# Attention on the array's sixteen squares: ten orders and divisions in place of one

## The chip, the cores and the metric

The kernel runs on one core of one Trainium2 chip. The metric is the device time of one execution in microseconds; shown is the median of three runs. Engines are called as in the profile: PE is the matrix engine (PEld its weight loads), DVE, ACT and POOL are the three element-wise engines, SP issues most of the DMAs.

## The reference

Cross attention with two sets of keys. There are 2 batches of 2048 tokens with 640 channels (20 heads of 32 channels), and per batch 154 context rows of 1024 channels: 77 text rows and 77 image rows. All numbers are float32.

```python
q = split_heads(x @ Wq.T, 20)
k, v = split_heads(text @ Wk.T, 20), split_heads(text @ Wv.T, 20)
out_text = merge_heads(softmax(q @ k.T / sqrt(32)) @ v)
k_ip, v_ip = split_heads(ip @ Wk_ip.T, 20), split_heads(ip @ Wv_ip.T, 20)
out_ip = merge_heads(softmax(q @ k_ip.T / sqrt(32)) @ v_ip)
return (out_text + out_ip) @ Wo.T + bo + x
```

## The kernel before

The 640 channels are five chunks of 128, and a chunk holds four heads. Chunk and batch together give ten numbers q = 0 to 9 (batch 0 first). For each q the kernel makes queries (`queries`, L201), scores of every token against the 154 keys of both sets (`scores`, L233), two softmaxes per head on DVE, POOL and ACT (`take` to `normalise`), a transpose of 32 x 32 blocks in place (`transpose`, L323), and then the weighted sum of the values on PE: `attend` (L332), called by the word `A.q` of the schedule. `take_attention` (word `CA.q`, L355 and L359, on ACT) copies its result from PSUM to the tile `aT`. The output projection (L471, L490, L500, L848) works on `aT`, for batch 0 beside the attention of batch 1, for batch 1 after it.

The order of all this is written out by hand, word by word, in `SCHEDULE`; each engine runs its own instructions in that order, and semaphores make it wait for the others. Nothing in the build chooses another order.

`attend` sees the PE array as sixteen squares of 32 rows and 32 columns. Square (r, g) works for head g of the chunk and for a quarter r of the tokens: its weights are the values `v4s[q % 2]` (tile `v`) of one key block, 32 keys by 32 channels, its moving operand are the probabilities of those keys in `pb` for 512 tokens (16 groups of 32 tokens), and it writes partitions 32g to 32g+31 of PSUM bank `pa[r]`. The 154 keys are padded to 160, five key blocks k = 0 to 4, which a square adds up in the same place of PSUM. That is 5 x 16 = 80 matmuls a call. A float32 matmul is run in two passes, each with its own weight load: four instructions (load, pass, load, pass), and two records of each kind in the profile. The 80 matmuls stand with the key block outermost, then the row r, then the column g ("by row").

The schedule gives each call half of the eight PSUM banks (`A.0@1` takes banks 4 to 7); their earlier contents must have been read by ACT or DVE before the first matmul that writes a bank.

Of the kernel before, what the change touches and what calls it, by code (L numbers as in the profile page):

```python
# [15 lines left out]
H, D, TEXT = 20, 32, 77  # L16
# [4 lines left out]
def kernel(  # L21
# [25 lines left out]
    nc = tc.nc  # L47
# [3 lines left out]
    G = P // D  # L51
# [9 lines left out]
    NK = (2 * L + D - 1) // D  # L61
# [28 lines left out]
    v4s = [const.tile([P, G, NK, D], F32, name=f"v4_{n}") for n in range(2)]  # L90
# [234 lines left out]
    def attend(q, pa):  # L325

        zones = pb[:, ds(q % 2, SUB)].rearrange("p z n g (k s) -> p (z n) g k s", k=NK)
        for k in range(NK):
            for r in range(G):
                rows = slice(r * D, (r + 1) * D)  # L330
                for g in range(G):
                    nc.tensor.matmul(  # L332
                        pa[r][g * D : (g + 1) * D, :],
                        v4s[q % 2][rows, g, k, :],
                        zones[rows, :, g, k, :],
                        start=(k == 0),
                        stop=(k == NK - 1),
                    )

    def rows_of_attention(b, c):  # L340

# [290 lines left out]
    def emit(word):  # L632
# [7 lines left out]
        elif k == "A":  # L640
            at[name] = halves[int(where)]
            attend(x, at[name])
        elif k == "CA":
            take_attention(x, at[f"A.{x}"])
# [246 lines left out]
```

## Time and profile before

| | us |
|---|---|
| median of three runs (497.68 to 497.79) | 497.76 |
| span of the profiled execution, first to last instruction | 496.7 |
| PE busy in it | 490.3 |
| PEld busy | 287.9 |
| DVE busy | 408.5 |
| POOL busy | 362.5 |
| ACT busy | 315.0 |
| `attend` (L332), PE busy, ten calls | 55.2 |

The profiled execution shows its span alone; the 1.06 us between the span and the median lie outside the instructions, and differences are reckoned against the median as they stand.

A profile line gives the source line, the engine, the operation and the tiles (`bank<-pb,v` reads pb and v and writes a bank). [...] "x160" counts records, so 160 are 80 matmuls. A weight load's line is PEld. In the view of stretches, each stretch has the busy time of an engine, and in brackets how many records lie in it or reach into it.

### The profile page before, as it was taken

Reading aid. Unit: us, or ns where it says so; the run is one execution under the profiler, and the core shown is the slowest. Engines: PE = TensorE matmul, PEld = TensorE weight load, DVE = VectorE, ACT = ScalarE, POOL = GpSimd, SP = SyncE. Lnnn points to the kernel's source line nnn. Section 1 sums busy time; section 2 is a strip of 40 time slices with the busy share of each in tenths; the row PEclk is TensorE's granted clock in tenths of the full one; section 3 lists DMA queues with packets and bytes.
Section 4 is the critical chain, followed back from the end, with each engine's and each line's share of the span. In section 5 each row is a group of like instructions: output and inputs, shape, how many; then the busy total and the mean of one; then the engine's idle time right before and its main releaser. Section 6 shows DMA issues by size and latency. Waiting matters only on the chain.

```text
span 496.7 us, 10482 instructions
## 1 busy us (share of the span) xinstructions
PE 490.3 (99%) x4114; PEld 287.9 (58%) x4114; DVE 408.5 (82%) x412; ACT 315.0 (63%) x1021; POOL 362.5 (73%) x157
## 2 busy tenths in 40 slices
PE   8999999999999999999999999999999999999997
PEld 5676657657547556456647654755755675444442
DVE  0069989979979989969976896687999978898877
ACT  1165878978978778668999786587578966100000
POOL 0069978798888999989874858565899888284830
PEclk9999999999999999999999999999999999999999
DMA  8991440332360454886445177418525401420115
GB/s 259 356 246 40 132 120 1 106 93 69 92 213 3 132 178 132 274 273 237 158 152 191 58 244 210 133 57 246 174 69 171 127 23 43 149 84 1 43 73 223
DMA packets 67474, 69.38 MB, mean 140 GB/s; under 512 B 5473, under 2 KB 47201, under 8 KB 67425
## 3 DMA queue, kind: packets, MB, share of 16 engines
q1 hardware_dynamic: 66704, 68.00, 43.8%
q8 instruction: 32, 0.52, 0.5%
q10 hardware_dynamic: 720, 0.72, 0.4%
q14 instruction: 18, 0.14, 0.1%
HBM read 54.94 MB, written 10.49 MB: 132 GB/s over the span
## 4 chain that ended last, share of the span: by engine, by line
PE 92%; DMA 3%; SPq 1%; DVE 1%; POOL 1%; ACT 1%; issue 0%; POOLq 0%
PE bank L201 33%; PE bank L848 11%; PE bank L490 10%; PE bank L233 10%; PE bank L332 10%; PE bank L142 9%; PE bank L471 6%; PE bank L500 3%; DMA aT<-in_L_xattn_Wk_ip_dram 2%; DMA wq<-in_L_xattn_Wq_dram 2%; SPq L534 1%; POOL pb L316 1%; DVE den L306 0%; ACT pb L301 0%; SPq L132 0%
## 5 line engine op out<-in xcount | busy, mean ns | idle before, releaser
L316 POOL TENSOR_TENSOR pb<-pb,rden 128x1848 f32<-128x1848 f32 (+1 forms) x60 | 176.1, 2944 | 39.7 <-DVE rden L311 35.5
L201 PE MATMUL bank<-x,wq 128*128 128x512 f32 x400 | 180.4, 601 | 0.6 <-DMA x<-in_x_dram 0.5
L295 POOL TENSOR_TENSOR pb<-pb,mx 128x1848 f32<-128x1848 f32 (+1 forms) x38 | 119.3, 3152 | 51.8 <-DVE mx L281 51.5
L201 PEld LDWEIGHTS bank<-x,wq 128*128 128x128 f32 x400 | 74.1, 191 | 86.7 <-issue 80.8
L323 DVE STREAM_TRANSPOSE pb<-pb 128x1920 f32<-128x1920 f32 (+1 forms) x60 | 115.7, 1932 | 4.9 <-POOL pb L316 4.3
L281 DVE TENSOR_REDUCE mx<-pb 128x24 f32<-128x1848 f32 (+1 forms) x51 | 93.7, 1850 | 30.7 <-ACT pb L245 30.5
L245 ACT COPY pb<-bank 128x462 f32<-128x462 f32 (+1 forms) x204 | 87.2, 539 | 36.0 <-PE bank L233 35.4
L306 DVE TENSOR_REDUCE den<-pb 128x24 f32<-128x1848 f32 (+1 forms) x47 | 88.7, 1895 | 17.6 <-ACT pb L301 13.3
L301 ACT ACTIVATE pb<-pb 128x1848 f32<-128x1848 f32 (+1 forms) x38 | 64.2, 1696 | 17.8 <-POOL pb L295 17.5
L269 ACT ACTIVATE pb<-pb,mx 128x77 f32<-128x77 f32 x224 | 67.8, 364 | 0.3 <-DVE mx L281 0.2
L233 PEld LDWEIGHTS bank<-kT,qT 32*128 32x128 f32 x1280 | 45.4, 184 | 26.9 <-issue 15.6
L269 ACT ACTIVATE pb<-bank,mx 128x77 f32<-128x77 f32 x184 | 51.8, 386 | 9.3 <-DVE mx L284 9.3
L233 PE MATMUL bank<-kT,qT 32*128 32x154 f32 x1280 | 56.2, 305 | 0.3 <-ACT kT L559 0.3
L332 PE MATMUL bank<-pb,v 32*32 32x512 f32 x1600 | 55.2, 597 | 0.0
L142 PE MATMUL bank<-wo_ct,aT 128*128 128x154 f32 x320 | 45.6, 296 | 0.3 <-DMA aT<-in_L_xattn_Wk_ip_dram 0.3
L142 PEld LDWEIGHTS bank<-wo_ct,aT 128*128 128x128 f32 x320 | 42.9, 188 | 3.6 <-issue 2.2
L332 PEld LDWEIGHTS bank<-pb,v 32*32 32x32 f32 x1600 | 29.9, 103 | 22.8 <-issue 10.7
L211 ACT ACTIVATE qT<-bank 128x512 f32<-128x512 f32 x40 | 24.2, 619 | 22.1 <-PE bank L201 22.0
L471 PE MATMUL bank<-aT,wo_ct 128*128 128x512 f32 x80 | 36.1, 596 | 0.0
L269 ACT ACTIVATION_READ_ACCUMULATOR pb<-bank,mx 128x1 f32 x128 | 33.6, 267 | 0.0
L490 PE MATMUL bank<-aT,wo_ct 128*128 128x256 f32 x128 | 32.3, 385 | 0.0
L490 PEld LDWEIGHTS bank<-aT,wo_ct 128*128 128x128 f32 x128 | 23.7, 190 | 6.5 <-issue 3.0
(75 smaller groups left out, 434.4 us busy)
## 6 DMA issues: line engine op xcount, KB each, us to landing
x<-in_x_dram SPq DMA_DIRECT2D x20, 1280.0 KB, 6.7
out_dram<-acc SPq DMA_DIRECT2D x20, 256.0 KB, 2.3
x<-in_x_dram SPq DMA_DIRECT2D x18, 256.0 KB, 5.9
acc<-in_x_dram SPq DMA_DIRECT2D x16, 256.0 KB, 4.7
out_dram<-x SPq DMA_DIRECT2D x15, 256.0 KB, 2.0
v<-vS SPq DMA_DIRECT2D x160, 20.0 KB, 2.8
wq<-in_L_xattn_Wq_dram SPq DMA_DIRECT2D x9, 320.0 KB, 5.0
aT<-in_L_xattn_Wk_dram SPq DMA_DIRECT2D x5, 512.0 KB, 5.5
```

Of the source, the lines that this page charges most:

```text
L142: nc.tensor.matmul(keys_in(out), loaded[n][:, k, :], cT[:, k, :, t, :], start=(k == 0), stop=(k == NCC - 1))
L201: nc.tensor.matmul(pq, wqs[q % 3][:, k, :], xs[place_of(u, h)][:, k, :], start=(k == 0), stop=(k == NC - 1),)
L233: nc.tensor.matmul(ps[g][:, ts(t, 2 * L)], qTs[(u, h)][g * D : (g + 1) * D, ts(st, P)], kT[g * D : (g + 1) * D, c, b].rearrange("p t l -> ...
L245: nc.scalar.copy(keys_of(u, s)[:, :, g], ps[g][:, : n * 2 * L].rearrange("p (n l) -> p n l", n=n))
L269: nc.scalar.activation(row, row if ps is None else rows_in(ps[g], n)[:, t, x], AF.Exp, bias=maxs[(u, s)][:, *one], accum_out=None if den i ...
L281: nc.vector.tensor_reduce(mx, rows_of(u, s), AX.X, ALU.max, negate=negate)
L295: nc.gpsimd.tensor_tensor(rows_of(u, s), rows_of(u, s), maxs[(u, s)].unsqueeze(3).to_broadcast([P, n, 2, L]), ALU.subtract)
L306: nc.vector.tensor_reduce(den_of(u, s), rows_of(u, s), AX.X, ALU.add)
L316: nc.gpsimd.tensor_tensor(rows_of(u, s), rows_of(u, s), rdens[(u, s)].unsqueeze(3).to_broadcast([P, n, 2, L]), ALU.mult)
L323: nc.vector.transpose(p, p)
L332: nc.tensor.matmul(pa[r][g * D : (g + 1) * D, :], v4s[q % 2][rows, g, k, :], zones[rows, :, g, k, :], start=(k == 0), stop=(k == NK - 1),)
L490: nc.tensor.matmul(part, w_of[m][:, kp, op], t_of(m, b, i)[:, kp], start=(op == kp == 0 and m in (1, 2, 5)), stop=(op == 1 and kp == 1 and ...
```

## The change

Only `attend` is changed. Each q has its own entry of a table: an order of the sixteen squares (`byrow`, `bycol`, `diagonal`), and for each of the sixteen a number `first`. Where `first` is 32, the first key block is one matmul as before. Where it is between 2 and 32, the square's matmul of the first key block covers only the first `first` tokens of each group of 32 tokens, and the others follow as a matmul of their own after the last key block. Where it is 2, the two pieces (2 and 30 tokens of each group) follow each other at once. All sixteen squares still run every key block in the table's order. The products and sums are the same.

```diff
     def attend(q, pa):
 
         zones = pb[:, ds(q % 2, SUB)].rearrange("p z n g (k s) -> p (z n) g k s", k=NK)
-        for k in range(NK):
-            for r in range(G):
-                rows = slice(r * D, (r + 1) * D)
-                for g in range(G):
-                    nc.tensor.matmul(
-                        pa[r][g * D : (g + 1) * D, :],
-                        v4s[q % 2][rows, g, k, :],
-                        zones[rows, :, g, k, :],
-                        start=(k == 0),
-                        stop=(k == NK - 1),
-                    )
+        byrow = [(r, g) for r in range(G) for g in range(G)]
+        bycol = [(r, g) for g in range(G) for r in range(G)]
+        diagonal = [((d + g) % G, g) for d in range(G) for g in range(G)]
+        order, first = (
+            (byrow, [12 + i for i in range(16)]),
+            (bycol, [12 + i for i in range(16)]),
+            (byrow, [12 + 2 * (i // 2) for i in range(16)]),
+            (byrow, [D, 2] + [D] * 14),
+            (bycol, [D] * 16),
+            (diagonal, [12 + i for i in range(16)]),
+            (byrow, [D, 2] * 8),
+            (byrow, [16 + i // 2 for i in range(16)]),
+            (bycol, [12 + i // 4 * 5 for i in range(16)]),
+            (byrow, [12 + i // 4 * 5 for i in range(16)]),
+        )[q]
+
+        def part(k, i, lo, hi, start, stop):
+            r, g = order[i]
+            rows = slice(r * D, (r + 1) * D)
+            nc.tensor.matmul(
+                pa[r][g * D : (g + 1) * D, :].rearrange("p (n s) -> p n s", s=D)[:, :, lo:hi],
+                v4s[q % 2][rows, g, k, :],
+                zones[rows, :, g, k, lo:hi],
+                start=start,
+                stop=stop,
+                skip_group_check=True,
+            )
+
+        for i in range(G * G):
+            part(0, i, 0, first[i], True, False)
+            if first[i] == 2:
+                part(0, i, 2, D, False, False)
+        for k in range(1, NK):
+            for i in range(G * G):
+                part(k, i, 0, D, False, False)
+        for i in range(G * G):
+            if 2 < first[i] < D:
+                part(0, i, first[i], D, False, True)
```

A call of q = 0, 1, 2, 5, 7, 8 or 9 has 96 matmuls now, that of q = 6 has 88, that of q = 3 has 81 and that of q = 4 has 80. The other engines run the same instructions in the same order. The rows below are PE's instructions in program order, with what each waits for; `bank_71` to `bank_74` are PSUM banks 4 to 7, `v_0_80` and `v_1_81` are the two value tiles, `32x512` is a moving operand of 32 partitions and 512 columns, `32x16x12` one of 16 groups of 12.

The first key block of the call q = 0, before: sixteen whole matmuls by row.

```order
L332 MATMUL bank_71<-pb,v_0_80 32x512 [waits DMAHW0_49,DVE_49,Activation_49]
L332 MATMUL bank_71<-pb,v_0_80 32x512 [waits DMAHW4_49]
L332 MATMUL bank_71<-pb,v_0_80 32x512 [waits DMAHW6_49]
L332 MATMUL bank_71<-pb,v_0_80 32x512 [waits DMAHW2_49]
L332 MATMUL bank_72<-pb,v_0_80 32x512 [waits DMAHW1_49,Activation_49]
L332 MATMUL bank_72<-pb,v_0_80 32x512 [waits DMAHW5_49]
L332 MATMUL bank_72<-pb,v_0_80 32x512 [waits DMAHW7_49]
L332 MATMUL bank_72<-pb,v_0_80 32x512 [waits DMAHW3_49]
L332 MATMUL bank_73<-pb,v_0_80 32x512 [waits DMAHW2_49,Activation_49]
```

The same place now:

```order
L347 MATMUL bank_71<-pb,v_0_80 32x16x12 [waits DMAHW0_49,DVE_49,Activation_49]
L347 MATMUL bank_71<-pb,v_0_80 32x16x13 [waits DMAHW4_49]
L347 MATMUL bank_71<-pb,v_0_80 32x16x14 [waits DMAHW6_49]
L347 MATMUL bank_71<-pb,v_0_80 32x16x15 [waits DMAHW2_49]
L347 MATMUL bank_72<-pb,v_0_80 32x16x16 [waits DMAHW1_49,Activation_49]
L347 MATMUL bank_72<-pb,v_0_80 32x16x17 [waits DMAHW5_49]
L347 MATMUL bank_72<-pb,v_0_80 32x16x18 [waits DMAHW7_49]
L347 MATMUL bank_72<-pb,v_0_80 32x16x19 [waits DMAHW3_49]
L347 MATMUL bank_73<-pb,v_0_80 32x16x20 [waits DMAHW2_49,Activation_49]
```

Squares and waits stand where they stood; each matmul covers 12 to 27 columns of every 32.

The end of the call q = 1, before: the last key block by row, and then the scores that follow.

```order
L332 MATMUL bank_71<-pb,v_1_81 32x512 x4
L332 MATMUL bank_72<-pb,v_1_81 32x512 x4
L332 MATMUL bank_73<-pb,v_1_81 32x512 x4
L332 MATMUL bank_74<-pb,v_1_81 32x512 x4
L233 MATMUL bank_67<-kT,qT_0_752 128x154 [waits Activation_49]
```

The same place now:

```order
L347 MATMUL bank_74<-pb,v_1_81 32x16x9
L347 MATMUL bank_71<-pb,v_1_81 32x16x8
L347 MATMUL bank_72<-pb,v_1_81 32x16x7
L347 MATMUL bank_73<-pb,v_1_81 32x16x6
L347 MATMUL bank_74<-pb,v_1_81 32x16x5
L233 MATMUL bank_67<-kT,qT_0_768 128x154 [waits Activation_49]
```

What the first key block left out comes last, sixteen short matmuls in the order by column; five of these rows are shown.

The start of the call q = 6, before:

```order
L332 MATMUL bank_71<-pb,v_0_80 32x512 [waits DVE_49,Activation_49]
L332 MATMUL bank_71<-pb,v_0_80 32x512 [waits DMAHW1_49]
L332 MATMUL bank_71<-pb,v_0_80 32x512 x2
L332 MATMUL bank_72<-pb,v_0_80 32x512 [waits DMAHW6_49,Activation_49]
L332 MATMUL bank_72<-pb,v_0_80 32x512
```

The same place now:

```order
L347 MATMUL bank_71<-pb,v_0_80 32x512 [waits DVE_49,Activation_49]
L347 MATMUL bank_71<-pb,v_0_80 32x16x2 [waits DMAHW1_49]
L347 MATMUL bank_71<-pb,v_0_80 32x16x30
L347 MATMUL bank_71<-pb,v_0_80 32x512
L347 MATMUL bank_71<-pb,v_0_80 32x16x2
L347 MATMUL bank_71<-pb,v_0_80 32x16x30
L347 MATMUL bank_72<-pb,v_0_80 32x512 [waits DMAHW6_49,Activation_49]
```

Every second square has two matmuls one behind the other, and the first key block is 24 matmuls.

## The prediction

> **What bounds the kernel now.** The page first, for the engine that sets the end:
>
> ```profile
> span 496.7 us, 10482 instructions
> ...
> PE 490.3 (99%) x4114; PEld 287.9 (58%) x4114; DVE 408.5 (82%) x412; ACT 315.0 (63%) x1021; POOL 362.5 (73%) x157
> ...
> PE 92%; DMA 3%; SPq 1%; DVE 1%; POOL 1%; ACT 1%; issue 0%; POOLq 0%
> ...
> L332 PE MATMUL bank<-pb,v 32*32 32x512 f32 x1600 | 55.2, 597 | 0.0
> ```
>
> PE is busy for 490.3 of 496.7 us and carries 92% of the chain that ended last; the four lines before the last are its start. Next PE's row of waits, longest and shortest of five:
>
> ```profile
> PE bank L549 <- DVE pb L547: 1.1, 1, 1.1
> ...
> PE bank L490 <- DVE acc L515: 0.2, 1, 0.2
> ```
>
> The five sum to 2.2 us. So a microsecond that `attend` takes more or less on PE is a microsecond of the span, as long as PE waits for nobody else, and L332 holds 55.2 us. Third, inside one call (q = 2): the timeline of PE and of its weight loads.
>
> ```profile
> 143.97 5.52 PE L332 MATMUL bank<-pb,v 32*32 32x512 f32 x160
> 149.41 0.81 PE L233 MATMUL bank<-kT,qT 32*128 32x154 f32 x16
> ```
>
> ```profile
> 143.96 0.23 PEld L332 LDWEIGHTS bank<-pb,v 32*32 32x32 f32 x32 [0.76 <-ACT vT L688]
> 144.42 0.10 PEld L332 LDWEIGHTS bank<-pb,v 32*32 32x32 f32 x1 [0.23 <-issue]
> 144.85 0.55 PEld L332 LDWEIGHTS bank<-pb,v 32*32 32x32 f32 x32 [0.32 <-issue]
> 145.71 2.87 PEld L332 LDWEIGHTS bank<-pb,v 32*32 32x32 f32 x95 [0.30 <-issue]
> ```
>
> A call takes 5.52 us of PE. What could it take? The pace of a pass stands in these rows (two windows of PE):
>
> ```profile
> 248.53 6.17 PE L201 MATMUL bank<-x,wq 128*128 128x512 f32 x14
> ```
>
> ```profile
> 387.26 1.03 PE L490 MATMUL bank<-aT,wo_ct 128*128 128x256 f32 x4
> ```
>
> ```profile
> L332 PE MATMUL bank<-pb,v x1600: 584/587/612, 69.8 to 428.6; 32*32 32x512 f32 x178
> ```
>
> Fourteen passes of 512 columns: (6.17 - 0.59 for the last one's record) / 13 = 0.429 us each; four of 256 columns: (1.03 - 0.38) / 3 = 0.217. A pass costs by its columns with nearly nothing fixed, and a matmul, two passes, 1.676 ns per column: 0.858 us for 512. Were no square ever idle, five key blocks would take 5 x 0.858 = 4.29 us and not 5.52. Where the difference lies, the loads tell, counted by stretch over the same call:
>
> ```profile
> 143.96:144.40 0.44, 0.23 (x32) 1.00 1.10 360
> 144.40:144.80 0.40, 0.10 (x1) 1.00 1.12 347
> 144.80:145.02 0.22, 0.10 (x1) 1.00 1.18 342
> 145.02:145.46 0.44, 0.37 (x31) 1.00 0.99 264
> 145.46:145.87 0.41, 0.10 (x1) 1.00 0.51 136
> 145.87:146.10 0.23, 0.13 (x2) 1.00 0.23 60
> 146.10:146.50 0.40, 0.35 (x29) 1.00 0.33 70
> ```
>
> Sixteen matmuls are loaded at once (32 loads), then one load, the first square's for key block 1, and at about 144.85 that square goes on. The fifteen others end their second passes then too (0.86 after their start), and nothing is loaded for them until 145.04, 1.07 us after the call began. The next bunch comes another 1.07 us later. I read this as a store of 64 instructions, that is 16 matmuls of load, pass, load, pass, which empties in order: the 65th is admitted when the oldest has left, and a pass leaves at the end of its record, 0.587 after its start, 0.158 later than its square is free. So a matmul starts one matmul time and about 0.215 us (1.073 - 0.858) after the start of the seventeenth matmul ahead of it. Check: the 80th hangs on the 63rd, 46th, 29th and 12th. Four waits of 1.073, eleven steps of 0.017 inside the last bunch (15 matmuls take 0.25 us to be loaded, 31 loads in 0.37 less 0.10 for one), a first load of 0.026, then 0.858, make 5.36, and 0.158 more for the last record 5.52, as the row says.
>
> **The change, call by call.** The call's length goes by the chain of every seventeenth matmul: start, columns of the chain x 1.676 ns, 0.215 per wait. N matmuls have (N - 1) / 17 waits, rounded down: 4 for 80 and 81, 5 for 88 and 96. Before it is 5.36.
>
> *q = 0, 1, 2, 5, 7, 8, 9 (96 matmuls).* The chain that ends with the 96th is made of the 11th (a short first part of 22 x 16 = 352 columns), four whole ones and the last rest of 80: 2480 columns, 4.16 us, which is one short part less than 2560. The 11th starts at 0.09, five waits are 1.075: 5.33, so 0.03 less than before. The parts of unequal length do spread the squares' ends, but the admission in order is what binds, and it counts matmuls. For q = 1 and 5 that is -0.03; q = 2 ends on 96 columns (0.00); for 8 and 9 the bunches of four equal parts are slowed by the steps of 0.017 (-0.01 each). q = 7 has 336 + 2048 + 144 columns, 48 more, +0.08. In q = 0 and 7 the waits for the third and fourth bank cost too; their hold shows in the first call before, with matmuls under way by 0.11, 0.25 and 0.43 us:
>
> ```profile
> 69.77:69.88 0.11, 0.10 (x8) 1.00 1.28 298
> 69.89:70.02 0.13, 0.13 (x12) 1.00 1.25 303
> 70.03:70.20 0.17, 0.17 (x16) 1.00 1.18 283
> ```
>
> There the 9th to 12th start about 0.07 late. It cost nothing: four whole 1.073 steps covered it. With short first parts it stays in the chain, so +0.07 less the 0.03 for q = 0 (+0.04), and with the longer columns +0.12 for q = 7. Sum of the seven calls: +0.08.
>
> *Order alone (q = 4, and the order by column or diagonal in 1, 5, 8).* All four banks are needed by the first four matmuls instead of the first thirteen. They are free long before: the last readers of the banks of q = 1 and q = 8, each with the call behind it, are
>
> ```profile
> 102.47 1.89 ACT L245 COPY pb<-bank 128x462 f32<-128x462 f32 x4
> ...
> 106.88 1.72 PE L332 MATMUL bank<-pb,v 32*32 32x512 f32 x36
> ```
>
> ```profile
> 385.82 0.34 ACT L269 ACTIVATION_READ_ACCUMULATOR pb<-bank,mx 128x1 f32 x1
> ...
> 388.65 5.54 PE L332 MATMUL bank<-pb,v 32*32 32x512 f32 x160
> ```
>
> 2.5 us each. Cost 0.
>
> *q = 3 (81).* Four waits as before; the 81st hangs on the 13th, which starts one or two steps later: +0.03.
>
> *q = 6 (88).* The first sixteen places hold 16 of 24 matmuls of the first key block, so squares 11 to 15 begin a whole wait late, and the chain needs a fifth wait. By the chain: 0.026 + 1.073 + (480 columns, 0.805, + 0.215) + 3 x 1.073 + 0.09 for the last steps + 0.858 = 6.28. That is +0.92 us.
>
> *What no row prices: short runs.* A whole matmul reads 16 runs of 32 columns and keeps the pace of L201's unbroken 512, so breaks in the operand cost nothing there (0.858 in both). The parts read and write runs of 5 to 27, and every output row of this trace is unbroken. Lower end 0, and a gain is excluded since the same columns pass. Upper end: half pace for the parts, 432 columns of the chain once more, 0.72 us a call, 5.1 in seven. I take 0, the end that the 32-column row is nearest to. [...]
>
> *Beside PE.* 121 more matmuls are 484 more instructions on PE alone; no DMA or copy moves. In the seven calls all four banks end within some 0.2 us of each other, as by row, so ACT's copies begin when they did.
>
> **Sum.** +0.08 + 0.03 + 0.92 = +1.03, against the median 497.76: 498.8.
>
> **The rivals.**
> - *Short runs cost.* Same waits, but the parts run at up to half pace: up to 498.8 + 5.1 = 503.9, at a quarter more 500.1. For it: no row with a broken output. Against: the 32-column runs are free.
> - *The stagger works (the other side).* If the 0.215 pauses come from the squares being in step, so that all weights fall due together, and not from a store that empties in order, then unequal first parts end the pauses. Each of the seven calls loses four, 0.86 us: 497.76 - 6.0 = 491.8, and down to 490 if q = 3 and 6 gain as well. For it: in each pause fifteen squares are empty at the same time. Against: from the second bunch on the first square runs free, out of step, and the pauses stay 1.07 us apart and move on by just one matmul a time. It decides where the second bunch of loads of q = 1 follows the first by less than a part's time plus 0.2.
> - *The short pieces of q = 6 leave the store early*, so that its 88 matmuls need four waits like 81. Then that call costs +0.1 and the total is 498.0. Against: they stand behind a whole matmul, and the store empties in order.
>
> **How the numbers follow.** The forecast gets 0.55; with my small terms uncertain by 0.3 each way, and the unpriced ones only upward, its own range is 498.4 to 499.4. Short runs get 0.22, the stagger 0.11, cheap pieces 0.12. A measurement here tells 0.2%, 1.0 us, from nothing, and the forecast lies on that bound: I count 0.32 of its 0.55 as slower and 0.23 as the same. Slower: 0.32 + 0.22 + 0.02 = 0.56; same: 0.23 + 0.09 = 0.32; faster: 0.11 + 0.01 = 0.12. The range goes from 497.2, below the cheap-pieces case, to 502.5, short runs at some two thirds of their upper end; outside lie the stagger and the last part of the short runs, under 2 in 10.
>
> **What would show it.** In the changed profile, the call of q = 6 should hold PE for about 6.4 us (6.28 and the record's end) with a bunch of loads more, q = 4 for 5.52, and the seven calls between 5.4 and 5.7. In q = 6 the 34th and later loads should be missing until 1.07 us after its start. If the seven calls stand at 6 us or more with the same number of bunches, the short runs cost; if they stand at 4.7, the pauses went. The prediction is wrong if PE gets waits after `attend` that it had not, since nothing in it counts on them.

## The result, and the profile after

The changed kernel takes 499.21 us (median of 16 runs, 498.84 to 502.06); the kernel before 497.77 (median of 16 runs as well). The ratio is 1.0034, with a 95% interval of 1.0025 to 1.0043: slower by a third of a per cent, 1.44 us by the two medians, 1.2 to 2.1 us by the interval.

The page of the changed kernel, the lines that answer to those of before:

```profile
span 497.5 us, 10968 instructions
...
PE 491.8 (99%) x4356; PEld 298.1 (60%) x4356; DVE 408.8 (82%) x412; ACT 314.7 (63%) x1021; POOL 362.5 (73%) x157
...
q8 instruction: 34, 0.56, 0.5%
...
PE 94%; ACT 1%; DVE 1%; POOL 1%; DMA 1%; issue 0%; DVEq 0%
...
L347 PE MATMUL bank<-pb,v 32*32 32x512 f32 (+12 forms) x1842 | 57.1, 542 | 0.0
```

PE still carries the span. `q8` carries instructions, 16 KB at a time: 34 transfers now, 32 before. They are taken here for those of TensorE (another name for PE): of loads, passes, semaphore and drain instructions the trace lists 8800 for it now and 8315 before, that is 34 and 32 times 256 and a rest. That line was not read in the prediction, and it turned out to matter.

One row per call, q = 0 to 9, of PE's passes of L347 (`attend` in the changed kernel; in some kernels further down it is L349 or L353). Each window runs from the first pass of the call to the first pass of the line behind it, so the second column is the call's length. Then PE's busy time and its passes, PE's clock, and DMA's share and GB/s:

```profile
68.94:74.43 5.49, 5.49 (x192) 1.00 0.26 61
106.08:111.51 5.43, 5.42 (x192) 1.00 0.02 3
143.15:148.59 5.44, 5.44 (x192) 1.00 0.49 149
178.13:183.59 5.46, 5.46 (x162) 1.00 0.50 135
210.76:216.21 5.45, 5.45 (x160) 1.00 0.97 334
253.83:259.25 5.42, 5.42 (x192) 1.00 0.75 258
300.33:307.59 7.26, 7.26 (x176) 1.00 0.73 243
346.88:352.46 5.58, 5.58 (x192) 1.00 0.45 126
389.43:394.87 5.44, 5.44 (x192) 1.00 0.16 51
424.39:429.83 5.44, 5.44 (x192) 1.00 0.70 217
```

The same windows of the kernel before for q = 0, 6 and 8 (the other seven are within 2 ns of q = 0, to the trace's nanosecond 5.448 to 5.450 us):

```profile
69.78:75.23 5.45, 5.45 (x160) 1.00 0.30 73
...
301.17:306.62 5.45, 5.45 (x160) 1.00 0.70 241
388.65:394.13 5.48, 5.48 (x160) 1.00 0.26 85
```

Nine calls changed by 0.13 us or less. One, q = 6, went from 5.45 to 7.26. To the nanosecond the ten differences sum to 1.91 us; from the start of the first call to the end of the last the two profiles differ by 1.58 us, so 0.34 is won back between calls. Of that, 0.31 lies at one place, behind q = 6. In the profile before, PE waits there for DVE; in the profile after, which comes to this line later, it does not:

```profile
312.41 1.13 PE L490 MATMUL bank<-aT,x 128*128 128x256 f32 x4 [0.24 <-DVE acc L515]
```

```profile
313.08 1.13 PE L517 MATMUL bank<-aT,x 128*128 128x256 f32 x4
```

From the start of the last pass ahead of it to that of this one it is 0.53 us before and 0.22 after. (The first call began 0.84 us earlier in the profile after, 68.94 for 69.78, where PE's waits for DMAs sum to 0.2 us for 0.8; that is why the spans differ by 0.8 only.)

What PE does in q = 6, from the timeline of its weight loads (start, length, loads, and in brackets the idle time before):

```profile
300.33 0.28 PEld L347 LDWEIGHTS bank<-pb,v 32*32 32x32 f32 x33 [0.76 <-ACT pb L269]
300.98 0.10 PEld L347 LDWEIGHTS bank<-pb,v 32*32 32x32 f32 x1 [0.36 <-issue]
301.40 0.38 PEld L347 LDWEIGHTS bank<-pb,v 32*32 32x32 f32 x33 [0.33 <-issue]
302.02 0.10 PEld L347 LDWEIGHTS bank<-pb,v 32*32 32x32 f32 x1 [0.23 <-issue]
302.42 3.39 PEld L347 LDWEIGHTS bank<-pb,v 32*32 32x32 f32 x105 [0.30 <-issue]
306.62 0.14 PEld L347 LDWEIGHTS bank<-pb,v 32*32 32x32 f32 x3 [0.80 <-issue]
307.59 0.30 PEld L498 LDWEIGHTS bank<-aT,wo_ct 128*128 128x128 f32 x2 [0.84 <-ACT aT L382]
```

The second bunch starts 1.07 us after the first, at 301.40, as forecast (a single load, the 34th, comes at 300.98). But at the call's end, with 173 of 176 loads done, there are no loads from 305.71 to 306.62 (the last one before the hole starts at 305.714), and three stragglers follow. The store of 64 instructions doesn't explain that: half of the call's extra time is something else.

### The profile page after: what moved, and what is told of

The parts are those of the page before. It is cut to its first block, busy times and chain, and to the rows that moved or that the text cites. A ratio compares the mean times of both kernels' runs of the same rounds, so it can differ in the third digit from the quotient of the medians.

```text
span 497.5 us, 10968 instructions
## 1 busy us (share of the span) xinstructions
PE 491.8 (99%) x4356; PEld 298.1 (60%) x4356; DVE 408.8 (82%) x412; ACT 314.7 (63%) x1021; POOL 362.5 (73%) x157
## 4 chain that ended last, share of the span: by engine, by line
PE 94%; ACT 1%; DVE 1%; POOL 1%; DMA 1%; issue 0%; DVEq 0%
PE bank L201 34%; PE bank L875 11%; PE bank L347 11%; PE bank L517 10%; PE bank L233 10%; PE bank L142 8%; PE bank L498 7%; PE bank L527 3%; DMA wq<-in_L_xattn_Wq_dram 1%; POOL pb L295 1%; DVE mx L281 1%; ACT pb L245 0%; POOL pb L316 0%; ACT aT L386 0%; DVE pb L323 0%; ACT pb L301 0%
## 5 line engine op out<-in xcount | busy, mean ns | idle before, releaser
L347 PE MATMUL bank<-pb,v 32*32 32x512 f32 (+12 forms) x1842 | 57.1, 542 | 0.0
L347 PEld LDWEIGHTS bank<-pb,v 32*32 32x32 f32 x1842 | 40.2, 103 | 19.3 <-issue 7.3
```

The source lines that it names most:

```text
L347: nc.tensor.matmul(pa[r][g * D : (g + 1) * D, :].rearrange("p (n s) -> p n s", s=D)[:, :, lo:hi], v4s[q % 2][rows, g, k, :], zones[rows, : ...
```

## The experiments

Theory A is the prediction's: a store of 64 instructions that empties in order, one wait of 0.215 us for each 17 matmuls on the chain. Its rivals were a fixed price per matmul, a price for short runs, and pauses that a stagger would end. For the hole in q = 6 two readings were open: that pairs themselves cost it, or that TensorE waited there for its next instructions (called the block theory here; the "theory B" of the first expectation is the other reading, the pairs). A time given without an interval is that of one run.

### Pairs in every call, and their number

All ten rows of the table as that of q = 6; the first is shown:

```diff
-            (byrow, [12 + i for i in range(16)]),
+            (byrow, [D, 2] * 8),
...
```

> All ten calls have the division of q = 6 (every second square's first key block as 2 and 30 tokens of each group, 88 matmuls). The call of q = 6 took 7.26 us up to the next line's first pass, where the call before takes 5.45; the forecast was 6.37, and 0.90 of the rest is a hole near its end, in which one second pass and the last matmul wait until the array is empty. Theory A (the store of 64 instructions alone, the hole an accident of where that call stands in the instruction stream): nine or ten calls take 6.37 and only one or two have the hole; total about 498 + 9 to 11 = 507 to 509. Theory B (the hole belongs to the division: the last bunch has only three matmuls, and the next line's load of another shape enters the store while they are still to be loaded): all ten calls take 7.26, total about 498 + 18 = 516. Rival C (each extra matmul has a fixed price, 0.92 / 8 = 0.115 us): 6.37 in all ten as well; the next run tells it from A.

Measured: 508.61 us, against 497.43 of the kernel before. Calls of 6.42, 6.43, 6.37, 7.21, 7.86, 6.37, 6.37, 6.42, 6.43 and 6.37 us. Eight stand at 6.37 to 6.43, 0.92 to 0.98 over before; two, q = 3 and 4, have a hole each. q = 6 has none here, though it is the same sixteen squares in the same order that took 7.26 in the changed kernel. The hole of q = 3, in the timeline of the loads:

```profile
182.90 1.20 PEld L347 LDWEIGHTS bank<-pb,v 32*32 32x32 f32 x37
185.62 0.24 PEld L347 LDWEIGHTS bank<-pb,v 32*32 32x32 f32 x31 [1.53 <-issue]
```

The second kernel asks whether the number of matmuls or the number of waits sets the price. All calls go by column, and the first p squares are in two parts of 2 and 30 columns, p being 1, 2, 3, 4, 5, 6, 7, 8, 12 and 16 from call to call (the ten entries are written here as one):

```diff
+            (bycol, [2] * p + [D] * (16 - p)),
```

> By column, with the first 1, 2, 3, 4, 5, 6, 7, 8, 12 and 16 squares divided into 2 and 30 tokens, for q = 0 to 9: 81 to 88, 92 and 96 matmuls. Store of 64 instructions that empties in order: the length to the next line against 5.45 is +0.01 to 0.05, +0.02 to 0.09, +0.04 to 0.14, then +0.25, +0.47, +0.68, +0.90 (one wait more builds up from the 83rd to the 87th matmul), +0.91, and then nearly level, +0.97 to 1.03 and +1.03 to 1.15. A fixed price per extra matmul (0.115): +0.12, 0.23, 0.35, 0.46, 0.58, 0.69, 0.81, 0.92, 1.38, 1.84, a straight line. If the hole before the end comes with a short last bunch, it adds 0.9 in the calls with 86 to 88 matmuls (last bunch of one to three) and not in those with 81 to 84, 92 and 96.

Measured: 504.83 us. The calls' excess over the same call before, for 81 to 88, 92 and 96 matmuls: 0.01, 0.03, 0.11, 0.32, 0.47, 0.69, (2.49), 0.92, 0.95, 1.04 us. The one in brackets has a hole of 2.4 us. A fixed price per matmul would be a straight line, 0.115 for each of the first eight; instead the second part costs 0.02, the fourth 0.22, and the eight from the 88th to the 96th cost 0.12 together. That is how theory A has it, where a part is dear if it puts a square's start behind one more wait.

### Short runs

All calls go by column, and the operand is cut at the same number of columns in two ways. For an even q the cut runs through every group of 32 columns (runs of 2 to 30, output rows broken), for an odd q between groups (unbroken):

```diff
+            if q % 2:
+                out, mov = out[:, lo // 2 : hi // 2], mov[:, lo // 2 : hi // 2]
+            else:
+                out, mov = out[:, :, lo:hi], mov[:, :, lo:hi]
```

The calls 2i and 2i + 1 have the same first parts: unequal ones of 12 to 26 columns in 32 in the first two calls, then for all sixteen squares 16, 4, 2 and 30 columns in 32.

> By column. Calls in pairs with the same numbers of columns: the even q cuts the first key block inside each group of 32 tokens (broken runs in PSUM), the odd q cuts between whole groups (unbroken runs). q = 0, 1: first part 12 to 26 thirty-seconds; q = 2, 3: 16; q = 4, 5: 4 (runs of 4 and 28); q = 6, 7: 2 (runs of 2 and 30, the rest at the end of the call); q = 8, 9: 30. If broken runs cost nothing, both of a pair take the same: 5.45 for the first pair and +0.20 for the four others (one wait more). [...]

Measured: 503.05 us. Broken and unbroken: 5.445 and 5.444 us; 5.653 and 5.653; 5.652 and 5.653. In the last two pairs one of each has a hole (8.86 and 5.655; 5.655 and 6.41) and the clean ones stand at 5.655. Broken runs cost 1 ns in a call at most. The 0.20 us over 5.45 in equal parts is one wait more, as theory A has it. For broken runs of 2 to 30 floats, all even in number, the pairs of calls here show no slowing. The hole of q = 6, the longest of all:

```profile
303.04 0.64 PEld L353 LDWEIGHTS bank<-pb,v 32*32 32x32 f32 x12 [0.26 <-issue]
306.77 0.24 PEld L353 LDWEIGHTS bank<-pb,v 32*32 32x32 f32 x32 [3.10 <-issue]
```

### First parts that rise steeply

By theory A the waits can be hidden in part if the first parts rise from very short to whole. All ten calls alike, with 94 matmuls:

```diff
+            (bycol, [3, 4, 6, 7, 7, 13, 15, 17, 18, 21, 25, 27, 30, 30, 32, 32]),
```

> All ten calls by column with the first parts 3, 4, 6, 7, 7, 13, 15, 17, 18, 21, 25, 27, 30, 30, 32, 32 of 32 tokens, that is 94 matmuls and a steeper stagger than 12 to 27. Store of 64 instructions: five waits as with 96, but the chain that ends last has fewer columns, since all seventeen chains are made nearly equally long: 5.22 us a call to the next line in place of 5.45, ten calls 2.3 us less, total 495.5 (ratio 0.9954). If the stagger as such were of no use or short runs cost, 5.4 to 5.5 a call and a total of 497.5 to 498.5. If something off PE takes the gain back, the calls are 5.22 and the total falls by less than 1.

Measured: 500.4 us (499.0 to 501.86), ratio 1.0064, interval 1.0043 to 1.0086: slower, where it should have been faster. Per call, q = 1 and q = 6:

```profile
105.83:111.13 5.30, 5.30 (x188) 1.00 0.02 6
...
300.73:308.22 7.49, 6.22 (x188) 1.00 0.62 203
```

Eight calls do get shorter, 5.31 us for 5.45: 0.14 each, where 0.23 was expected. What takes the rest, no run settles. The trace shows one thing for which the theory has no term of its own: the two passes of a matmul on one square start some 0.027 us further apart than their columns take (in q = 1, 0.067 us for 48 columns, 0.080 for 64, 0.107 for 96). But q = 2 takes 6.43 and q = 6 takes 7.49, with holes of 1.25 and 2.29 us: two holes eat more than eight gains.

### The changed kernel without its pairs

q = 6 whole and by row as before, and q = 0 and 7, which waited for banks, by column:

```diff
-            (byrow, [12 + i for i in range(16)]),
+            (bycol, [12 + i for i in range(16)]),
...
-            (byrow, [D, 2] * 8),
-            (byrow, [16 + i // 2 for i in range(16)]),
+            (byrow, [D] * 16),
+            (bycol, [16 + i // 2 for i in range(16)]),
```

> The changed kernel with q = 6 whole by row as before, and q = 0 and q = 7 by column instead of by row with their own first parts. If the pairs of q = 6 and the bank waits of q = 0 and 7 are the whole loss: q = 6 takes 5.45 again, q = 0 falls from 5.50 to 5.42 (as q = 1 has), q = 7 from 5.58 to 5.50, the other seven stay within 0.01 of what the changed kernel shows, and the ten calls sum to within 0.05 us of before: ratio 1.000. If the 96-matmul calls cost the kernel something outside themselves, it stays slower by up to 0.5 us. If instructions can come late here too, a call that is not q = 6 has a hole of 0.5 us or more.

Measured: 497.75 us against 497.48, ratio 1.0006, interval 0.9996 to 1.0015: the same as before. Calls: 5.425, 5.423, 5.445, 5.466, 5.450, 5.423, 5.450, 5.513, 6.116, 5.442. By column q = 0 is 0.02 shorter than before, where by row it was 0.05 longer, and q = 7 goes from 5.58 to 5.51. The order by column asks for all four banks within four matmuls, so it is not that the third and fourth bank came free late. The trace of the changed kernel shows what lengthens q = 0 by row, two semaphore instructions on TensorE inside the call (window 68.94 to 74.43):

```profile
L347 PEldq EVENT_SEMAPHORE  x2: 51/51/51, 69.0 to 69.1; - x2
```

Each takes 51 ns, the least of all 25 in this line, so neither seems to wait; but one stands in front of the ninth first pass and one in front of the thirteenth, which start 0.080 and 0.119 us behind the one before them, where the others are 0.007 apart. By column the same two stand 1.38 and 1.26 us ahead of the call's first pass, beside the matmuls of the line before, and the sixteen first passes start within 0.10 us. In q = 7 it is the same, with one such instruction ahead of the call by column. And the hole has gone from q = 6 to q = 8, 0.76 us, a call that this edit does not touch. Here are its loads in the two us before the transfer of 16 KB that it waited for (389.21 us; DMA's share and GB/s stand last), and those behind the hole:

```profile
387.20:389.20 2.00, 1.22 (x68) 1.00 0.00 0
```

```profile
391.52 0.56 PEld L347 LDWEIGHTS bank<-pb,v 32*32 32x32 f32 x33 [0.66 <-issue]
```

The DMA engines were idle.

### A bulk load away, a load moved, a half block put in front

Each hole ended 1.2 to 1.5 us after a transfer of 16 KB on `q8`. In fourteen of the sixteen holes counted further down, that of q = 6 among them, the DMA engines had been 0.91 busy or more in the two us before that transfer; in q = 9 of the kernel of short runs it was 0.49, and in q = 8 just shown next to nothing. So the 1.28 MB load of x ahead of q = 6 (half of the last chunk's input, unit 17) was left out:

```diff
     def load_block(u, h):
+        if (u, h) == (17, 1):
+            return
```

> The changed kernel without one load: the 1.28 MB of tokens that SP issues at 297.6 us, before the call of q = 6, are not fetched (the queries of the last chunk's second half use what the buffer held). In the changed kernel the DMA engines are full from 300 to 304 us, a 16 KB transfer of PE's own instructions starts at 304.18 when they become free, and the hole in q = 6 ends at 306.62. Theory (PE ran out of instructions because that transfer stood behind the load): the instruction transfer comes some microseconds earlier, the hole is gone, q = 6 takes 6.37 (7.26 before), and the other nine calls stay as they were. If the hole belongs to the division or to the store, q = 6 stays at 7.26.

Measured: 499.84 us; q = 6 7.65 us, its hole 305.83 to 307.13. The expectation failed. The windows of its loads say why it was no test: DMA's share is in the last column but one.

```profile
302.00:303.00 1.00, 0.53 (x33) 1.00 0.85 269
303.00:304.00 1.00, 0.69 (x33) 1.00 1.10 365
304.00:305.00 1.00, 0.68 (x37) 1.00 0.87 258
```

The next load of SP's queue, the unit's other half, had simply come forward.

Then the steep table in nine calls, q = 2 whole, and the same load of x put just ahead of its other half in SP's queue:

```diff
-        "... S1.14 LX.17.1 SS.1.4 ... cq.15.1 LX.17.0 ..."
+        "... S1.14 SS.1.4 ... cq.15.1 LX.17.1 LX.17.0 ..."
```

> The steep stagger (5.31 us a call where no instructions came late) in nine calls, q = 2 whole by row, and the 1.28 MB load that SP issued just before the call of q = 6 now behind that call's stores and fetches, so that it goes out about 8 us later. Theory: nine calls at 5.31, q = 2 at 5.45, no hole in q = 6, so 9 x 0.14 = 1.3 us less than before, total about 496.1, ratio 0.9975, if the shifted blocks bring no hole to another call; each hole takes 0.5 to 2.3 of it back. If the load's new place makes the queries wait for it (PE at about 326 us), the gain is lost there.

Measured: 500.96 us, ratio 1.0072, interval 1.0055 to 1.0089. Seven of the nine steep calls are 5.305 to 5.461 us, and three calls have holes: q = 2 (6.19, though whole), q = 3 (6.82) and q = 6 (6.83). Moving one load did not cure q = 6, and leaving q = 2 whole did not cure q = 2.

The third kernel shifts the whole program by half a block: 32 matmuls of two columns, 128 instructions, at the start.

```diff
+    for _ in range(32):
+        nc.tensor.matmul(banks[0][:, :2], warm, warm[:, :2], start=True, stop=True)
```

> The changed kernel with 32 more matmuls of 2 columns at the start, 128 more instructions, half of a 16 KB block, so that every block of 256 instructions ends half a block elsewhere; the start becomes later by some microseconds, and everything after it alike. Theory (late instructions): nine calls keep their lengths within 0.02 us, q = 6 keeps the store's 6.37 but its hole moves or goes, or another call gets one. If the hole belongs to the division: q = 6 takes 7.26 again, with the hole in the same place.

Measured: 515.04 us. Most of that is the matmuls themselves, which took far more than their columns, 0.213 us a pass (timeline of PE), the same as the passes of 128 columns just ahead of them (L576):

```profile
4.20 13.65 PE L578 MATMUL bank<-pb 128*128 128x2 f32 x64
```

The calls tell more. All are as in the changed kernel within 0.011 us, but q = 3 (6.17 for 5.47) and q = 6 (8.11 for 7.26). The hole of q = 6:

```profile
317.37 1.29 PEld L347 LDWEIGHTS bank<-pb,v 32*32 32x32 f32 x41 [0.30 <-issue]
320.69 0.24 PEld L347 LDWEIGHTS bank<-pb,v 32*32 32x32 f32 x32 [2.03 <-issue]
```

It opens after 109 loads of the call in place of 173: 64 loads, 128 instructions earlier. Counted from the program's start, it is the same instruction.

### Where the holes open

That count can be made for every hole: four instructions for each matmul ahead of it (load, pass, load, pass), two for each load of the call before it, and the 26 to 84 semaphore and drain instructions that the trace lists for TensorE ahead of it. Sixteen holes of 0.7 us and more, in ten kernels; n is the number of the first instruction behind the hole, counted from 0, and the last columns are when the last transfer of `q8` ended and when loads went on:

```
kernel                call    n     n = 256 x b + r   transfer ended   loads go on   later by
steep                 q=2   2754     10 x 256 + 194       145.54        146.89       1.35
steep, load moved     q=2   2754     10 x 256 + 194       145.88        147.24       1.36
steep, load moved     q=3   3521     13 x 256 + 193       182.23        183.63       1.40
all pairs             q=3   3522     13 x 256 + 194       184.16        185.62       1.46
shifted               q=3   3778     14 x 256 + 194       196.07        197.51       1.44
all pairs             q=4   4289     16 x 256 + 193       219.35        220.69       1.34
number of pairs       q=6   5825     22 x 256 + 193       307.03        308.27       1.24
changed kernel        q=6   6081     23 x 256 + 193       305.17        306.62       1.45
runs                  q=6   6081     23 x 256 + 193       305.55        306.77       1.22
steep                 q=6   6081     23 x 256 + 193       304.87        306.36       1.49
one load away         q=6   6081     23 x 256 + 193       305.67        307.13       1.45
shifted               q=6   6081     23 x 256 + 193       319.41        320.69       1.28
steep, load moved     q=6   6081     23 x 256 + 193       307.10        308.39       1.29
two loads away        q=6   6081     23 x 256 + 193       305.17        306.57       1.40
without pairs         q=8   7617     29 x 256 + 193       390.13        391.53       1.40
runs                  q=9   8642     33 x 256 + 194       432.01        433.45       1.44
```

The remainder is 193 or 194 every time. So in these traces a hole opened where TensorE was at the end of a block of 256 instructions and the next block had only just come, or not yet. The transfers go with that step: 34 of 16 KB for the 8800 instructions of the changed kernel (34 x 256 = 8704), 32 for the 8315 of the kernel before (32 x 256 = 8192). From load to load the sixteen holes are 0.7 to 3.2 us.

The block theory can now say beforehand where a hole can open, and the last four kernels try that. (Their expectations count without the semaphore instructions; the edge 6020 to 6022 there is n = 6081 here, and 5764 to 5766 is 5825.)

### The pairs alone, with the blocks elsewhere

The kernel before, written as a table of ten entries that are whole and by row, with q = 6 alone in pairs:

```diff
             (byrow, [D] * 16),
-            (byrow, [D] * 16),
+            (byrow, [D, 2] * 8),
             (byrow, [D] * 16),
```

> The kernel before with the pairs of query-chunk call q=6 alone (88 matmuls there, the nine other calls whole and by row). The store theory gives this call 6.36 to 6.42 us and the kernel +0.92 to +0.97 us, about 498.4. What separates the two readings of the other 0.9 us that this call took in the changed kernel: if the pairs themselves cost it (a form of the hardware's that the store theory lacks), the call is 7.2 to 7.3 us here too, and the kernel about 499.3. If it is a block of 256 instructions that came late, it depends on where the block's edge lies: counted in the program of TensorE (4 instructions to a matmul), all the holes so far began at an instruction whose number is about 256 times a whole number plus 118 to 168, drifting slowly down; near this call the edge is at 6020 to 6022, or 256 earlier, 5764 to 5766. This call holds the instructions 5416 to 5768, so that edge lies at its last matmul or two, and only those can wait: the call 6.4 to 6.9 us.

Measured: 498.72 us against 497.67, ratio 1.0025, interval 1.0015 to 1.0035. The call takes 6.372 us, the nine others 5.448 to 5.474 as before. No hole, not even at the last matmuls: the block of the edge at the call's last instruction had landed at 304.42, 2.1 us before TensorE came to it. The pairs by themselves cost the call 0.92 us, what theory A gave, and nothing else.

### A call undone, forty-six microseconds away

The changed kernel with q = 5 as before, 64 instructions fewer:

```diff
-            (diagonal, [12 + i for i in range(16)]),
+            (byrow, [D] * 16),
```

> The changed kernel with call q=5 alone as before (whole, by row: 80 matmuls for 96). The store theory by itself gives +0.027 us for q=5 and nothing elsewhere. The block theory says that the 64 instructions fewer move the edge 6020 to 6022 of the program from the 346th instruction of the 352 of call q=6 to the 410th, which is behind its end: no hole in q=6, which takes 6.34 to 6.42 us in place of 7.26, although nothing in it or near it is changed; the whole about 0.85 us below the changed kernel, 498.3 to 498.5. In q=8 an edge comes to the 278th of 384 instructions: a hole of up to 0.5 us may open there. Against the block theory speaks q=6 at 7.2 us or more again.

Measured: 498.41 us against 497.67, ratio 1.0013, interval 1.0003 to 1.0023. The end of q = 6 now:

```profile
302.30 3.44 PEld L347 LDWEIGHTS bank<-pb,v 32*32 32x32 f32 x108 [0.30 <-issue]
306.58 0.30 PEld L498 LDWEIGHTS bank<-aT,wo_ct 128*128 128x128 f32 x2 [0.84 <-ACT aT L382]
```

108 loads without a break where there were 105, a hole and 3. q = 6 takes 6.375 us for 7.26, though nothing in it was edited, and the 0.03 us that q = 5 had won are lost (5.453). The hole that could open in q = 8 did not (5.447).

### Why the block is late

Both loads of x of unit 17 left out, and then, since others came forward again, those too:

```diff
     def load_block(u, h):
+        if u == 17:
+            return
```

> The changed kernel without both loads of x of unit 17 (two halves of 1.28 MB each; the outputs of that unit come from old data). Taking away one alone left the hole in q=6 where it was, but the queue then simply went on to the other, and the DMA engines were still full (shares 0.85 and 1.10) in the two us before the block's transfer began. If the block comes late because its transfer waits behind bulk loads, it now starts before 303 us, there is no hole in q=6, and that call takes 6.34 to 6.42 us. If the block is asked for only when TensorE has come to a certain place, whatever the DMA engines do, the transfer starts at 304 to 305 us again and the call takes 7.2 to 7.7 us.

```diff
     def fetch(i, part):
+        if (i, PARTS.index(part)) in ((2, 4), (1, 2), (1, 3), (2, 0)):
+            return
```

> The changed kernel without both loads of x of unit 17 and without the four loads of 256 KB that came forward into their place (one into res, three into acc; the outputs that draw on these five places come from old data). With the two loads of x away alone, the DMA engines were still 0.83 to 1.06 busy from 301 to 304 us with those four, the block's transfer began at 304.25, when they were done, and call q=6 took 7.74 us. What is left here between 298 and 305 us is one store of 256 KB or two. If the block waits behind bulk transfers, its own transfer starts between 300.5 and 303 us, there is no hole, and q=6 takes 6.34 to 6.42 us. If it is asked for only at a place in TensorE's program, whatever the DMA engines do, it starts at 304 to 305 us for a third time and q=6 takes 7.2 to 7.7 us.

Measured: 499.35 and 497.85 us. q = 6 takes 7.74 us with two loads away, and 6.376 with the four others away too. The windows of the loads in q = 6 (loads, clock, DMA's share, GB/s), first of the changed kernel:

```profile
302.00:303.00 1.00, 0.62 (x33) 1.00 1.05 410
303.00:304.00 1.00, 0.70 (x33) 1.00 0.91 348
304.00:305.00 1.00, 0.66 (x33) 1.00 0.11 35
305.00:306.00 1.00, 0.54 (x8) 1.00 0.21 37
```

Two loads away:

```profile
302.00:303.00 1.00, 0.66 (x35) 1.00 1.06 372
303.00:304.00 1.00, 0.74 (x34) 1.00 0.96 311
304.00:305.00 1.00, 0.73 (x34) 1.00 0.20 66
305.00:306.00 1.00, 0.21 (x5) 1.00 0.68 173
```

All six away:

```profile
301.00:302.00 1.00, 0.47 (x34) 1.00 0.74 253
302.00:303.00 1.00, 0.73 (x34) 1.00 0.09 26
303.00:304.00 1.00, 0.69 (x34) 1.00 0.00 0
304.00:305.00 1.00, 0.71 (x34) 1.00 0.00 0
```

The block's transfer begins at 304.18, 304.25 and 302.66 us: within 0.7 us behind the point where the engines' share falls from about 1 to nearly nothing. (In the quiet kernel that point is the end of a store of 256 KB, near 302.) With the traffic gone it comes 1.5 us sooner, 1.1 us sooner counted from TensorE's passing the edge of the block before, and the hole is gone:

```profile
302.00 3.44 PEld L349 LDWEIGHTS bank<-pb,v 32*32 32x32 f32 x108 [0.30 <-issue]
306.29 0.30 PEld L501 LDWEIGHTS bank<-aT,wo_ct 128*128 128x128 f32 x2 [0.84 <-ACT aT L384]
```

So for q = 6 both conditions are shown: an edge of a block must lie in the call (the undone q = 5 takes it out), and bulk transfers must hold the block back (the quiet kernel, one run, takes most of them out; TensorE comes to the edge at 305.31 there, 1.73 us after the block has landed). For other holes the second is not shown: ahead of that of q = 8 in the kernel without pairs the engines were idle for two us, and yet the transfer began 2.66 us after TensorE had passed the edge before. What kept it there is open.

When a block is asked for can be read from the same count. In the changed kernel TensorE passes the edge before that of the hole (the first load at or behind n = 5825) at 301.52, and the transfer begins 2.66 us later; with two loads away 3.26, with all six away 1.56. Over the fourteen traces, for the blocks whose edge before lies in a call of `attend`: where the engines were idle in the two us before the transfer (share 0.05 or less, 45 blocks) it begins 0.1 us before TensorE passes that edge to 2.4 us after, 0.9 in the median; where they were full (0.9 or more, 83 blocks) 0.9 us before to 4.4 us after, 2.7 in the median. So in these calls a block is not fetched far ahead: it comes about when the one before it is begun, and later when the engines are full.

The kernel before has the same traffic, and its block of 305.23 is as late; but its edge (n = 5825, 256 earlier) lies 31 instructions behind the end of q = 6, behind ten passes of 512 columns that take 4.5 us.

No run was found that beats the kernel before: the best, the changed kernel without its pairs, is the same within its interval.

## Why the prediction was right, and where not

The forecast was 498.8 us, of its own range 498.4 to 499.4; measured 499.21, on the side of slower to which the most was given. By its steps:

- *The store that empties in order* held. Forecast and measured differences per call, in us: q = 0 +0.04 and +0.047; q = 1 -0.03 and -0.023; q = 2 0 and -0.005; q = 3 +0.03 and +0.017; q = 4 0 and 0; q = 5 -0.03 and -0.027; q = 7 +0.12 and +0.132; q = 8 -0.01 and -0.034; q = 9 -0.01 and -0.007. Only the absolute length was short, 5.36 for 5.45: it left out what stands between the call's last matmul and the next line's first pass.
- *The waits for the third and fourth bank*, which the terms for q = 0 and 7 drew on, had the right size and the wrong name: by column, with the banks asked for sooner, both calls are 0.07 shorter. What holds the passes back is two semaphore instructions inside the call, 51 ns each, and not banks that come free late.
- *Short runs* at 0, the end that was taken, is right to 1 ns in a call, for the even runs of that experiment. The half pace of the upper end was the author's assumption; no run shows it.
- *The stagger* as a way to end the pauses fell: the seven calls stand at 5.42 to 5.58, as admission in order has it. A steeper table does win 0.14 in a call, by shorter chains.
- *The short pieces of q = 6* did not leave early: its fifth wait is there, +0.92 for the pairs alone, to the hundredth.
- *q = 6* as a whole is where the sum is off: 1.81 for 0.92. The step that failed is "121 more matmuls are 484 more instructions on PE alone; no DMA or copy moves". 484 instructions are almost two blocks more to fetch, 34 transfers on `q8` for 32, and every edge between blocks behind the first call moves. One came to lie behind the 346th of the 352 instructions of q = 6, behind a burst of loads, and cost 0.89 us there.
- *A microsecond of `attend` is a microsecond of the span* did not hold behind q = 6: there PE's wait for DVE, the shortest of the five rows that the prediction drew on (L490 <- DVE acc), took up 0.31 us of the longer call. (The five rows sum to 2.4 us, not 2.2.)
- *The total*: 1.03 forecast, 1.91 by the calls, 1.58 with what came back between them, 1.44 by the medians. That the forecast lay so near is in part luck: the hole added 0.89 us that it did not have, and 0.34 us came back that it did not count on either.

The bound of 0.2% was drawn at 1.0 us, and the forecast lay on it; the hole put the result clearly behind it.

## What to carry to other kernels

Where TensorE runs 80 to 96 small matmuls in 5.4 to 5.6 us, as here, count instructions as well as columns: a chain of every seventeenth matmul priced nine of the ten calls to 0.03 us. Then look at the queue that brings the instructions: behind busy DMA engines in fourteen of the sixteen holes, and once behind idle ones, a block came late here, and whether that cost anything hung on where the edges fell, 256 instructions apart: undoing q = 5 took 0.89 us off q = 6. A per-call table of lengths, before and after, shows this at once; a total does not. And look at what stands behind an edited stage: a wait there, such as PE's for DVE behind q = 6, takes up part of what the stage loses, here 0.31 of 1.81 us.

## What the runs showed of the hardware

- TensorE stopped at 16 edges of 256 instructions (numbers 193 and 194 behind a multiple of 256), for 0.7 to 3.2 us, and went on 1.22 to 1.49 us after the transfer of the block had ended.
- In q = 6 the transfer of a block began as bulk transfers ended: at 304.18 and 304.25 us behind bursts that ended near 304, and at 302.66 where they ended near 302. In q = 8 of the kernel without pairs it began 2.66 us after TensorE had passed the edge before, with the DMA engines idle for the last two of these.
- In the calls of `attend` a block's transfer began 0.9 us (median of 45) after TensorE passed the edge before where the DMA engines were idle, 2.7 us (median of 83) where they were full, and never more than 0.9 us before it.
- The two passes of a matmul on one square of 32 by 32 started their columns' time and about 0.027 us apart: 0.067 us for 48 columns, 0.107 for 96.
- A semaphore instruction of 51 ns (the least that one took) among the first matmuls of a call held the next pass back to 0.080 or 0.119 us where others follow by 0.007.
- A two-column pass over 128 by 128 weights took 0.213 us, sixty-four in a row (13.65 us), where 512 columns take 0.429.
